# Sorting earlier and pacing attention from unit 5's first product in a one-core graph attention kernel

## The chip, the cores and the metric

The kernel runs on one NeuronCore of a Trainium2 chip. The metric is the device time of one execution in microseconds (us). Engines are called as the profile calls them: PE (TensorE, the matmul engine), DVE (VectorE), ACT (ScalarE), POOL (GpSimd) and SP (SyncE, which here only issues transfers). ACT, SP and POOL each have a DMA queue.

## What is computed

`x` has 2708 rows (nodes) of 1024 features, `adj` is a 2708 × 2708 matrix of zeros and ones, with an edge probability of 0.0014771, so that a row has about four edges.

```
h = max(layernorm(x), 0)
q = h @ W_q.T + b_q;  k = h @ W_k.T + b_k;  v = h @ W_v.T + b_v
z = (q @ k.T) / sqrt(1024) * adj
z = where(z == 0, -10000, z)
out = x + relu(softmax(z, axis=1) @ v)
```

Everything is float32.

## The kernel before

**Algebra.** `q @ k.T` is `(h @ M) @ h.T` with `M = W_q.T @ W_k / sqrt(1024)` and a bias row. So the kernel forms M, then rows `q' = h @ M + b`, and a row's scores are dot products of its q' with those few rows of h that are its neighbours. The weighted sum u of these rows of h is multiplied by `W_v.T` last, so that there are two dense stages of 2708 × 1024 × 1024 and no dense attention.

**The search.** DVE finds the columns of the ones of each row tile of `adj` (128 rows) by a search over four quarters (`found`), and `listed` turns the finds of a batch of up to four tiles into up to 16 keys per row. `counts` counts the keys, `sort` works out with two small matmuls at which position a row comes in an order by falling degree, and `put` scatters the rows' tables to that place; `reload` brings the sorted table back. Rows 0 to 1023 (tiles 0 to 7, searched last, in two batches of four) are one part, and the others, searched first, another. After the sort, tile t needs only K[t] gathered neighbours: 8 (and one row of sums kept elsewhere), 7, 5, 5, 4, 3, 3, 2 for tiles 0 to 7. Tile 21 stands for the neighbours of tiles 0 and 8 beyond the eighth, and has 7.

**Units.** The dense work is done in 20 units of two row tiles (256 rows) and one single tile. Units 0 to 9 ("q") form q' of tiles 0 to 19, units 10 to 19 ("o") form the output of the tiles in the order of attention. A unit does seven block products of the Strassen-Winograd scheme in place of eight, written by `multiply(n, results, after)` in this order (`multiply` calls `after(i)` between them, i being the step; the work of the other engines is written there):

- after steps 0 and 1: `s2` by T1 (bank Y); step 2; `a12` (bank X), then `c11`; step 3; `s4` (bank Z), then `c12`; step 4; `s3` (bank Y), then `c22`; step 5; then for the next unit `a11` and `s1` (`between` and `opened`); then `a22` (bank Y), then `c21`; step 6.

The result `c22` reads bank Y, which the `a22` product writes next. In q units of tiles 8 to 11 and in all o units but the last, ACT first copies the bank (`copied`); in the other q units DVE reads the bank itself (L1091). The operands `s1` to `s4` of unit n + 1 are sums on DVE (`blocks`: `upper` transposes the first tile, `lower` the second and does the sums, L722), written in steps 0 and 2 of unit n, and for unit 4 in steps 4 and 5 of unit 3. PE transposes the tiles, except o tiles that were stored in a turned order (`faced_tiles`), which DVE transposes (L705). A q unit's rows are gathered by POOL two units ahead (`load_rows`), and q' of tiles 8 to 19 is stored to `q_late` (L1084). Unit FIRST = 4 is the first whose rows come sorted; `last_q` is 9.

**Attention.** `attention(order)` is a generator that runs beside units 5 to 18. The order of the tiles is 6, 5, 4, 3, 2, 21, 0, 20, 7, 17, 13, 18, 12 and so on. For each tile `fetch` loads its rows of q' on POOL (L833 for tiles from 8 on, which waits for their store), `fill` gathers neighbours into the 11 buffers that are free (L610), `scores` does K[t] dot products on DVE (L863), `weights` the softmax, `sums` adds the weighted rows on DVE (L923). Scores of the next tile stand before the sums of this one where both fit into the buffers. Tile 17 has 3 neighbours, tile 20 has 1.

**Pacing.** The generator yields an estimate after each operation: 1.3 for a score or a sum, 0.6 for a tile's weights. `advance(share)` writes out operations until their estimates use up what was granted. Each step grants `share`, 20.9 / 7 in units up to 14, less 2.3 / 7 for each tile of a following o unit that DVE transposes. Before unit n + 2's rows are loaded, `advance(1.0)` goes on until its tiles are done. From unit 4 on the order of DVE alone is the written one; the order of the other engines is the scheduler's. POOL's queue is in the scheduler's order too: an instruction that can go is put ahead of one that has to wait.

**Where the change touches.** `steps_at` and `steps_ahead` say which steps of search and sort are written in which (unit, step): "j21" is `listed(21)`, the keys of the last batch, "c0" its `counts`, "o0" its `sort`, "g0" to "g4" are sums of squares on ACT, "w0-7" the scatters, "b0" the reload. `steps_ahead` are followed at the start of a step, `steps_at` near its end.

Of the kernel before, what the change touches and what calls it, by code (L numbers as in the profile page):

```python
# [65 lines left out]
def tile_preln_masked_attention(  # L66
# [147 lines left out]
    def stats(group):  # L214

        G = len(group)
        mv = stat.tile([P, 4, 2], FT, tag="mv", name="mv")
        if tiles[group[-1]][1] < P:
            nc.vector.memset(mv, 1.0)
        xs = []  # L220
        for i, t in enumerate(group):
            t0, n = tiles[t]
            if 15 <= t < 18:
                xt = work.tile([P, D], FT, tag="q", name=f"x_{t}", bufs=4)
            elif t >= FULL - 1:
                xt = work.tile([P, D], FT, tag="hT", name=f"x_{t}", bufs=2)
            else:
                xt = row_tile(f"x_{t}")
            if t < EARLY:
                kept[t] = xt  # L230
            nc.sync.dma_start(xt[:n], x[t0:t0 + n, :])
            xs.append(xt)
            if t in MOMENTS:
                continue
            st = stat.tile([P, NH, 6], FT, tag="st", name="st")
            for s in range(NH):
                nc.vector.bn_stats(st[:n, s, :], xt[:n, s * NB:(s + 1) * NB])
            nc.vector.bn_aggr(mv[:n, i, :], st[:n].rearrange("p s k -> p (s k)"))
        normed[group[0]] = group, xs, mv

    def moments(t):

        group, xs, mv = next(g for g in normed.values() if t in g[0])
        i = t - group[0]
        junk = work.tile([P, D], mybir.dt.uint8, tag="junk", name="junk_x", bufs=1)
        nc.scalar.activation(junk, xs[i], AF.Copy, scale=-1.0 / (ROOT * D), accum_out=mv[:, i, 0:1])
        nc.scalar.activation(junk, xs[i], AF.Square, scale=1.0 / ROOT, bias=mv[:, i, 0:1], accum_out=mv[:, i, 1:2])
# [3 lines left out]
    def root(first):  # L251

        group, xs, mv = normed.pop(first)
        G = len(group)
        r = stat.tile([P, 5, 4], FT, tag="r", name="r")
        mean, var = mv[:, :G, 0], mv[:, :G, 1]
        down = float(ROOT) if first in MOMENTS else -1.0
        eng = nc.gpsimd
        eng.tensor_scalar(r[:, 0, :G], var, EPS, None, op0=ALU.add)
        eng.tensor_tensor(r[:, 1, :G], r[:, 0, :G], minus[:, :G], op=ALU.pow)  # L260
        eng.tensor_tensor(r[:, 2, :G], r[:, 0, :G], r[:, 1, :G], op=ALU.mult)
        eng.tensor_tensor(r[:, 2, :G], r[:, 2, :G], r[:, 1, :G], op=ALU.mult)
        eng.tensor_scalar(r[:, 2, :G], r[:, 2, :G], -0.5, 1.5, op0=ALU.mult, op1=ALU.add)
        eng.tensor_tensor(r[:, 3, :G], r[:, 2, :G], r[:, 1, :G], op=ALU.mult)
        eng.tensor_scalar(r[:, 2, :G], mean, down, None, op0=ALU.mult)
        rooted.append(eng.tensor_tensor(r[:, 4, :G], r[:, 2, :G], r[:, 3, :G], op=ALU.mult))  # L266
        eng.tensor_scalar(msq[:, 9 + group[0]:9 + group[0] + G], r[:, 3, :G], MLIMIT / THIN, None, op0=ALU.mult)
        normed[first] = group, xs, r
# [40 lines left out]
    def follow(steps):  # L309

        for step in steps.split():
            first, *only = step[1:].split(".")
            first, *last = first.split("-")
            first = int(first or 0)
            if step[0] == "s":
                stats(range(first, int(last[0] if last else first) + 1))
            elif step[0] == "m":
                moments(first)
            elif step[0] == "r":
                root(first)  # L320
            elif step[0] == "a":
                apply(first, *[range(int(o[0]), int(o[-1]) + 1) for o in only])
            elif step[0] in "hk":
                keep(first, step[0] == "h")
            elif step[0] == "+":
                owe(first)
            elif step[0] == "p":
                counted(first)
            elif step[0] == "c":
                counts(*halves[first])  # L330
            elif step[0] == "o":
                sorted_at.append(sort(*halves[first]))
            elif step[0] == "w":
                pooled.close()
                with tc.issue_after((behind if first < EARLY else products)[-1].ins):
                    entered.append(put(first, int(last[0]) + 1))
            elif step == "z":
                pooled.enter_context(tc.manual_schedule(engines={mybir.EngineType.Pool}))
                with tc.issue_after(entered[-1].ins):
                    reload(EARLY, NT)  # L340
            elif step[0] == "b":
                reload(*halves[first])
            elif step[0] == "g":
                squared(first)
            else:
                if step[0] == "e":
                    counted(first)
                if step[0] != "j":
                    found(first, *[range(int(o[0]), int(o[-1]) + 1) for o in only])
                if step[0] != "i":  # L350
                    listed(first)
# [262 lines left out]
    rows_of = {}  # L614
    FIRST = EARLY // 2
# [147 lines left out]
    def natural_rows(n):  # L763
# [23 lines left out]
    steps_ahead = {(1, 5): "o1", (3, 6): "o0"}  # L787

    slots, free = [], []

# [217 lines left out]
    def add_block(bank, a, b, last=True):  # L1008
        for c in range(4):
            mm = nc.tensor.matmul(bank, a[:, c, :], b[:, c, :], start=False, stop=(c == 3), skip_group_check=True)  # L1010
        return mm
# [3 lines left out]
    def opened(n):  # L1015

        if n not in banks_of:
            return
        X, Z = banks_of[n]
        ops = ops_of[n][0]  # L1020
        add_block(X, ops["a11"], M[:, 0, 0])
        Y = psum.tile([P, NB], FT, tag="acc", name="psy")
        nc.scalar.copy(Y, X)
        products.append(add_block(Z, ops["s1"], T[:, 0] if units[n][0] == "q" else M[:, 0, 1]))
        p5 = small("p5")
        nc.scalar.copy(p5, Z)
        opened_of[n] = Y, p5
# [168 lines left out]
    units = [("q",) + p for p in q_pairs] + [("o",) + p for p in o_pairs]  # L1196
# [20 lines left out]
    last_q = len(q_pairs) - 1  # L1217
# [13 lines left out]
    for n, unit in enumerate(units):  # L1231
# [5 lines left out]
            nc.sync.dma_start(bp_dram, bp_sb[0:1, :])  # L1237
        turn = n in (0, FIRST - 1)
        share = (20.9 if n < len(units) - 5 else 21.5) / 7
        nxt = units[n + 1] if n + 1 < len(units) else None  # L1240
        if nxt is not None and nxt[0] == "o":
            share -= 2.3 / 7 * len(set(nxt[1:]) & faced_tiles)
# [2 lines left out]
        def after(i):  # L1245
# [4 lines left out]
            if (n, i) == (2, 5):  # L1250
# [5 lines left out]
                owe(7)  # L1256
                rows_of[FIRST + 1] = load_rows(units[FIRST + 1])
                pooled.close()
            if n == FIRST and i in (1, 4, 5):
                for g in slots[:4] if i == 1 else slots[4:6] if i == 4 else slots[6:8]:  # L1260
                    with tc.issue_after(sorted_at[-1].ins):
                        nc.vector.memset(g, 0.0)
            b11, t1, b21, b22 = M[:, 0, 0], M[:, 0, 1], M[:, 1, 0], M[:, 1, 1]
# [24 lines left out]
                marked(EARLY, NT)  # L1288
            if (n, i) == (FIRST + 2, 4):
                nc.vector.tensor_scalar(msq, msq, MLIMIT, None, op0=ALU.is_gt)  # L1290
            if n > FIRST + 1 or n == FIRST + 1 and i > 1:
                advance(share)
            if nxt is not None:

                if i == (3 if n == 0 else 4 if turn else 0):
                    ops_of[n + 1] = blocks(*rows_of[n + 1], nc.gpsimd if n + 1 < FIRST - 1 else None)
                    with tc.issue_after(products[-1].ins) if n + 1 == FIRST else nullcontext():
                        ops_of[n + 1][1]()
                if i == (4 if n == 0 else 5 if turn else 2):
                    ops_of[n + 1][2]()  # L1300
                    rows_of.pop(n + 1)
                    if n == last_q - 1:
                        all_rows()
                if i == 3:
                    banks_of[n + 1] = banks_for(bp_sb)
                if i == 6 and n + 2 < FIRST:
                    natural_rows(n + 2)
                if i == (2 if n == FIRST else 3 if n == last_q else 4) and n + 2 > FIRST and n + 2 < len(units) and n + 2 not in rows_of:
                    while units[n + 2][0] == "o" and not done.issuperset(units[n + 2][1:]):
                        advance(1.0)  # L1310
                    rows_of[n + 2] = load_rows(units[n + 2])
# [259 lines left out]
```

## Time and profile before

| | |
|---|---|
| median of 3 runs | 635.72 us |
| runs | 635.58 to 637.35 us |
| the profiled execution | 631.83 us |
| its span in the trace | 630.1 us |
| granted TensorE clock, mean | 0.999 |
| busy: PE, DVE, ACT, POOL | 619.6, 523.3, 288.4, 363.1 us |
| transfers | 182.19 MB, mean 289 GB/s |

The times of the parts below are those of the profiled execution, from the start of its span. PE is busy almost throughout: the q units take 25.8 us each with their transposes, the o units 24.0 us. Unit 3's first own product begins at 190.4 us, unit 5's at 242.9, unit 9's at 346.9 and unit 10's at 371.0. A product is eight records of matmuls (four float32 matmuls of two passes) and takes 3.43 us.

A row of the timeline gives start, duration, engine, line, operation, output and inputs with their shapes, how many, and in brackets how long the engine sat idle before it and what ended that. A row of the chain of waits gives start, duration and what it was. A row of the transfers gives what was moved, the queue, how many, the size and the time from issue to landing. `psy` is bank Y, `ps` the banks X and Z, `wlow` holds T, `pq` is a tile's q' and `g` a gathered neighbour.

### The profile page before, as it was taken

The numbers are of one execution on the slowest core, as the hardware profiler recorded it, in microseconds if no ns is written. First come the engines' busy times: TensorE is split into PE (matmuls) and PEld (weight loads), VectorE is DVE, ScalarE is ACT, GpSimd is POOL, SyncE is SP. The second block draws the span as 40 slices with busy tenths as digits, with TensorE's granted clock in tenths as the row PEclk, the third lists the DMA queues.
The fourth block names the chain that finished last, engine by engine and source line by source line (L and its number), as shares of the span: only waits on it lengthen the run. The fifth ranks groups of instructions, "written<-read, shape, count | busy, mean of one in ns | idle before, by whom it ended". The sixth has DMA issues, their size and how long they took to land.

```text
span 630.1 us, 6067 instructions
## 1 busy us (share of the span) xinstructions
PE 619.6 (98%) x1579; PEld 310.3 (49%) x1579; DVE 523.3 (83%) x1022; ACT 288.4 (46%) x421; POOL 363.1 (58%) x394
## 2 busy tenths in 40 slices
PE   8999999999999999999999998999999999999996
PEld 5777766444444444454454443444444444444442
DVE  5999879997996664887988969999997999988741
ACT  3538985749677563343341333434342323343300
POOL 2649860885778177754561632757667477852241
PEclk9999999999999999999999999999999999999999
DMA  8999997688796439997489998899999999997481
GB/s 330 407 371 326 343 354 294 209 288 326 255 387 241 166 113 319 350 379 236 154 306 325 332 359 265 235 333 346 347 318 324 344 278 305 349 284 194 103 296 71
DMA packets 65088, 182.19 MB, mean 289 GB/s; under 512 B 9959, under 2 KB 20023, under 8 KB 64408
## 3 DMA queue, kind: packets, MB, share of 16 engines
q0 software_dynamic: 26656, 86.02, 43.4%
q1 hardware_dynamic: 31594, 71.53, 32.8%
q10 hardware_dynamic: 6798, 24.20, 9.8%
q8 instruction: 14, 0.23, 0.2%
q14 instruction: 26, 0.21, 0.1%
HBM read 146.70 MB, written 43.36 MB: 302 GB/s over the span
## 4 chain that ended last, share of the span: by engine, by line
PE 56%; DMA 17%; DVE 11%; issue 9%; POOL 4%; ACT 1%; SPq 1%; POOLq 0%; DVEq 0%; ACTq 0%
PE ps L1010 22%; PE psy L1010 15%; PE ps_y L476 7%; DMA out_dram<-y,tab 5%; PE ps_x L476 4%; DMA or<-u_dram 4%; PE ps_z L476 4%; DVE junk L863 4%; PE pt L415 3%; DMA pq<-q_late 2%; DVE u L923 2%; DMA q_late<-q 2%; DMA g<-h_dram,tab 2%; DMA u_dram<-v 1%; DVE a L705 1%
## 5 line engine op out<-in xcount | busy, mean ns | idle before, releaser
L1010 PE MATMUL psy<-wlow,s 128*128 128x512 f32 x320 | 144.0, 592 | 0.0
L1010 PE MATMUL ps<-M,a 128*128 128x512 f32 x320 | 144.0, 593 | 0.0
L610 POOL DMA_INDIRECT g<-h_dram,tab x91 | 110.3, 1212 | 55.8 <-ACT u L912 19.8
L863 DVE SCALAR_TENSOR_TENSOR junk<-g,pq 128x1024 uint8<-128x1024 f32 x90 | 110.0, 1223 | 16.8 <-DMA g<-h_dram,tab 10.2
L1010 PE MATMUL ps<-M,s 128*128 128x512 f32 x240 | 108.0, 592 | 2.2 <-DVE s L722 2.2
L1010 PEld LDWEIGHTS psy<-wlow,s 128*128 128x128 f32 x320 | 59.9, 190 | 72.4 <-issue 70.2
L1010 PEld LDWEIGHTS ps<-M,a 128*128 128x128 f32 x320 | 59.9, 190 | 71.8 <-issue 71.3
L923 DVE SCALAR_TENSOR_TENSOR u<-g,coef,u 128x1024 f32<-128x1024 f32 x66 | 84.6, 1282 | 4.9 <-ACT u L912 3.5
L1010 PEld LDWEIGHTS ps<-M,s 128*128 128x128 f32 x240 | 45.4, 190 | 59.7 <-issue 58.3
L389 DVE FIND_INDEX8 at<-ones,adj 128x8 uint32<-128x685 f32 (+1 forms) x88 | 74.5, 865 | 0.0
L1010 PE MATMUL psy<-wlow,a 128*128 128x512 f32 x160 | 72.0, 593 | 0.1
L368 ACT ACTIVATE sized<-adj 128x2708 uint8<-128x2708 f32 (+1 forms) x22 | 54.3, 2466 | 7.5 <-DMA adj<-in_adj_dram 6.1
L298 POOL TENSOR_TENSOR hsum<-hsum,x 128x256 f32<-128x256 f32 (+1 forms) x56 | 38.7, 728 | 25.4 <-DVE wlow L444 22.0
L1109 POOL DMA_INDIRECT y<-in_x_dram,tab x19 | 32.2, 1696 | 31.4 <-ACT y L1126 22.4
L1010 PEld LDWEIGHTS psy<-wlow,a 128*128 128x128 f32 x160 | 30.3, 190 | 38.7 <-issue 37.3
L944 ACT COPY v<-u 128x1024 f32<-128x1024 f32 x19 | 19.9, 1045 | 48.9 <-DVE u L923 43.5
L808 POOL DMA_INDIRECT out_dram<-y,tab x21 | 27.8, 1325 | 22.0 <-issue 13.6
L1010 PE MATMUL ps<-wlow,s 128*128 128x512 f32 x80 | 36.0, 592 | 0.0
L626 POOL DMA_INDIRECT tab_dram<-tab,pos_i x22 | 21.9, 993 | 20.9 <-DVE pos_i L689 15.4
L912 ACT ACTIVATE u<-g,coef 128x1024 f32<-128x1024 f32 x18 | 20.7, 1148 | 24.2 <-DVE coef L911 24.1
L760 ACT COPY ps<-bp_sb 128x512 f32<-128x512 f32 x42 | 24.6, 595 | 11.0 <-DVE y L1144 10.3
L276 ACT ACTIVATE x<-x,r 128x1024 f32<-128x1024 f32 (+1 forms) x22 | 25.8, 1232 | 5.6 <-POOL r L266 5.6
(251 smaller groups left out, 848.5 us busy)
## 6 DMA issues: line engine op xcount, KB each, us to landing
adj<-in_adj_dram SPq DMA_DIRECT2D x21, 1354.0 KB, 11.2
x<-in_x_dram SPq DMA_DIRECT2D x21, 512.0 KB, 4.2
h_dram<-x ACTq DMA_DIRECT2D x21, 512.0 KB, 8.4
u_dram<-v ACTq DMA_DIRECT2D x19, 512.0 KB, 8.5
or<-u_dram SPq DMA_DIRECT2D x76, 128.0 KB, 9.7
q_late<-q SPq DMA_DIRECT2D x12, 512.0 KB, 9.4
pq<-q_late POOLq DMA_DIRECT2D x12, 512.0 KB, 10.5
M<-in_wv_dram SPq DMA_DIRECT2D x3, 1024.0 KB, 15.4
```

Source lines behind the costliest of these rows:

```text
L276: nc.scalar.activation(xs[i][:n], xs[i][:n], AF.Relu, bias=r[:n, 4, i:i + 1], scale=r[:n, 3, i:i + 1])
L298: small.append(nc.gpsimd.tensor_add(hsum[:n, cols], hsum[:n, cols], xt[:n, cols]))
L368: nc.scalar.activation(sized[:n], a[:n, :, :PW], AF.Abs, accum_out=total[:n, t:t + 1])
L389: nc.vector.max_index(at[:n, k - first_k, g, :], ones[:n, 0:8], a[:n, g, :])
L476: mm = nc.tensor.matmul(bank, a_tile(o + H * a[0], a[1], i), b(o), start=first and o == 0, stop=(o == H - 1), skip_group_check=True)
L610: return nc.gpsimd.indirect_dma_start(out=dst, out_offset=None, in_=src, in_offset=off, bounds_check=N - 1, oob_is_err=False)
L760: nc.scalar.copy(return_[h], row[:, h * NB:(h + 1) * NB])
L808: to = nc.gpsimd.indirect_dma_start(out=out, out_offset=bass.IndirectOffsetOnAxis(ap=ptab.bitcast(U32)[:n, t, SLOTS:SLOTS + 1], axis=0), i ...
L863: chained(lambda: nc.vector.scalar_tensor_tensor(junk, g_of[t][s], 1.0, tq[t], op0=ALU.mult, op1=ALU.mult, accum_out=zall[:, t, s:s + 1]))
L923: chained(lambda: nc.vector.scalar_tensor_tensor(u, g_of[t][s], coef[:, s:s + 1], u, op0=ALU.mult, op1=ALU.add))
L1010: mm = nc.tensor.matmul(bank, a[:, c, :], b[:, c, :], start=False, stop=(c == 3), skip_group_check=True)
L1109: return nc.gpsimd.indirect_dma_start(out=y[:n], out_offset=None, in_=x, in_offset=off, compute_op=ALU.add)
```

## The change

Six things change:

- The keys and counts of the last batch ("j21 c0") are written in step 4 of unit 3, ahead of unit 4's sums; it was step 5, behind them. The squares "g0" stay in step 5.
- The sort "o0" is written inside `opened(4)`, between unit 4's `a11` and `s1` products; it was step 6 of unit 3.
- The eight buffers cleared on DVE are all cleared in step 1 of unit 4; it was four there, two in step 4 and two in step 5.
- `advance(share)` begins with step 0 of unit 5; it was step 2.
- Unit 9 is granted 2.3 less and unit 10 4.6 less, spread over their seven steps.
- The rows of units 6 to 9 are gathered in step 2 of the unit two before; for units 7, 8 and 9 it was step 4.

```
-                (3, 1): "i21", (3, 3): "p21", (3, 5): "j21 c0 g0", (3, 6): "w0-7 g1 g2 g3 g4", (4, 4): "b0"}
-    steps_ahead = {(1, 5): "o1", (3, 6): "o0"}
+                (3, 1): "i21", (3, 3): "p21", (3, 4): "j21 c0", (3, 5): "g0", (3, 6): "w0-7 g1 g2 g3 g4", (4, 4): "b0"}
+    steps_ahead = {(1, 5): "o1"}
...
         Y = psum.tile([P, NB], FT, tag="acc", name="psy")
         nc.scalar.copy(Y, X)
+        if n == FIRST:
+            follow("o0")
         products.append(add_block(Z, ops["s1"], T[:, 0] if units[n][0] == "q" else M[:, 0, 1]))
...
         share = (20.9 if n < len(units) - 5 else 21.5) / 7
+        if n in (last_q, last_q + 1):
+            share -= 2.3 / 7 * (n - last_q + 1)
...
-            if n == FIRST and i in (1, 4, 5):
-                for g in slots[:4] if i == 1 else slots[4:6] if i == 4 else slots[6:8]:
+            if n == FIRST and i == 1:
+                for g in slots[:8]:
                     with tc.issue_after(sorted_at[-1].ins):
                         nc.vector.memset(g, 0.0)
...
-            if n > FIRST + 1 or n == FIRST + 1 and i > 1:
+            if n > FIRST:
                 advance(share)
...
-                if i == (2 if n == FIRST else 3 if n == last_q else 4) and n + 2 > FIRST and n + 2 < len(units) and n + 2 not in rows_of:
+                if i == (2 if FIRST <= n <= last_q - 2 else 3 if n == last_q else 4) and n + 2 > FIRST and n + 2 < len(units) and n + 2 not in rows_of:
```

## The prediction, made before the change was run

> **What bounds the kernel.** I read the page first, then PE's waits, PE's timeline around the one large wait, the chain that ended last before it, and VectorE (DVE), POOL and the transfers in the same stretch.
>
> ```profile
> span 630.1 us, 6067 instructions
> ...
> PE 619.6 (98%) x1579; PEld 310.3 (49%) x1579; DVE 523.3 (83%) x1022; ACT 288.4 (46%) x421; POOL 363.1 (58%) x394
> ```
>
> PE is busy for 619.6 of 630.1 us, and the change takes no product away. So it can win only what PE idles, and little of that lies in the stages that it touches:
>
> ```profile
> PE ps L1010 <- DVE s L722: 2.2, 1, 2.2
> ...
> PE ps L1010 <- DVE T_alone L705: 0.8, 1, 0.8
> ```
>
> ```profile
> 357.22 3.60 PE L1010 MATMUL psy<-wlow,s 128*128 128x512 f32 x8
> ...
> 367.52 3.60 PE L1010 MATMUL psy<-wlow,a 128*128 128x512 f32 x8
> ...
> 384.68 3.60 PE L1010 MATMUL ps<-M,a 128*128 128x512 f32 x8
> 390.44 3.67 PE L1010 MATMUL ps<-M,s 128*128 128x512 f32 x8 [2.16 <-DVE s L722]
> ```
>
> A product is eight such records, 3.43 us from one to the next. 357.22 is unit 9's `s3` product, 367.52 its `a22` product (the last of unit 9), 390.44 the `s1` product of unit 11, begun inside unit 10, which waited 2.16 us for VectorE's `s1`. That wait is all that a faster VectorE can give. Why was VectorE late? The chain says:
>
> ```profile
> 343.65 3.45 PE psy L1010 x8
> ...
> 347.73 10.06 DMA q_late<-q
> ...
> 357.83 0.47 issue
> ...
> 358.32 13.95 DMA pq<-q_late
> ...
> 372.38 0.09 DVE junk L863
> ```
>
> ```profile
> 365.73 0.68 DVE L1091 TENSOR_TENSOR q<-psy,p 128x512 f32<-128x512 f32 x1
> 366.33 1.22 DVE L863 SCALAR_TENSOR_TENSOR junk<-g,pq 128x1024 uint8<-128x1024 f32 x1
> ...
> 372.38 1.23 DVE L863 SCALAR_TENSOR_TENSOR junk<-g,pq 128x1024 uint8<-128x1024 f32 x1 [3.64 <-DMA pq<-q_late]
> ...
> 389.60 0.69 DVE L722 TENSOR_TENSOR s<-a,s 128x512 f32<-128x512 f32 x1
> ```
>
> Tile 17's q is made by unit 8's last product (ends 347.1), stored until 357.8, loaded again until 372.3. VectorE stood 3.64 us at tile 17's first score for it. So VectorE's lateness at 390 is not mere load: it is a transfer that starts at a time which PE sets, and which more VectorE time cannot hasten. Note what stands just ahead of that score: L1091 at 365.73, which reads unit 9's bank Y (`c22`), so that the `a22` product may write it at 367.52.
>
> **The change, part by part.** The search's end, the sort, the memsets:
>
> ```profile
> 200.92 0.69 DVE L1094 TENSOR_TENSOR q<-ps,u 128x512 f32<-128x512 f32 x1 [1.58 <-issue]
> ...
> 206.23 1.29 DVE L722 TENSOR_TENSOR s<-a,pt 128x512 f32<-128x512 f32 x2 [0.36 <-ACT a L718]
> ...
> 208.76 0.28 DVE L402 TENSOR_TENSOR cand<-first,at 128x128 f32<-128x128 f32 x1
> ...
> 213.27 0.22 DVE L669 TENSOR_SCALAR tab<-keys 128x128 uint32<-128x128 f32 x1
> 216.48 0.31 DVE L682 COPY sort<-ps_all 128x144 f32<-128x144 f32 x1 [2.99 <-PE ps_all L680]
> ...
> 218.79 0.17 DVE L689 CAST pos_i<-deg 128x8 uint32<-128x8 f32 x1
> 219.11 0.91 DVE L1262 MEMSET g<- 128x1024 f32 x1 [0.15 <-issue]
> ...
> 224.68 1.29 DVE L722 TENSOR_TENSOR s<-a,pt 128x512 f32<-128x512 f32 x2 [1.43 <-issue]
> ```
>
> ```profile
> 209.28 3.60 PE L1010 MATMUL ps<-wlow,s 128*128 128x512 f32 x8
> ```
>
> Keys and counts take 213.49 − 208.76 = 4.7 us. In front of unit 3's `c22` and unit 4's `s1`, they run from 201.6 to 206.3, into idle time; `c22` follows until 207.0, `s1` is done at 207.7, and PE wants it at 209.28: no cost while 1.6 us of cover last. The sort's two matmuls only change place; they read counts ready by 206.3. Should PE take them before unit 4's `a11` product, which begins 3.43 us ahead of 209.28, it could lose 206.3 − 205.85, so 0 to 0.5 us; I take 0. From the copy of the counts to the positions VectorE takes 218.96 − 216.48 = 2.5 us; begun at 209.7 it ends near 212.2 in place of 218.96, so POOL's puts, SP's reload and tile 6's gathers move up by up to 6.7 us. The eight memsets together (about 1.07 us each from start to start, from 212.3) end near 221, before the sums of 224.68: nothing. The rows of q gathered two steps sooner issue the same transfers; POOL's queue has them 2 × 1.3 us ahead of row gathers that stood before them, while
>
> ```profile
> 309.42 1.39 POOL L612 DMA_INDIRECT qr<-h_dram,tab  x1 [0.30 <-issue]
> ```
>
> ```profile
> qr<-h_dram,tab POOLq DMA_INDIRECT x1, 4.7
> ```
>
> ```profile
> 319.42 1.04 PE L415 MATMUL pt<-ident,qr 128*128 128x128 f32 x8
> ```
>
> the one issued at 309.4 landed 4.7 us later, at 314.1, for transposes at 319.4. The rows had 5 us to spare and get more: 0; 2.6 us more on POOL for a gather of the planner I price with the scores below.
>
> Attention from unit 5's first step:
>
> ```profile
> 240.75 1.23 DVE L863 SCALAR_TENSOR_TENSOR junk<-g,pq 128x1024 uint8<-128x1024 f32 x1 [5.17 <-DMA g<-h_dram,tab]
> ...
> 248.05 1.28 DVE L722 TENSOR_TENSOR s<-a,pt 128x512 f32<-128x512 f32 x2 [3.21 <-ACT a L718]
> ```
>
> ```profile
> 260.98 3.60 PE L1010 MATMUL ps<-wlow,s 128*128 128x512 f32 x8
> ```
>
> Scores begin between 234 (all 6.7 us gained) and 240.75 (none gained). By the planner's arithmetic below, seven scores and sums and one tile's weights then stand before the sums of 248.05, where three scores did: even from 240.75 and with 2.6 us of POOL's queue in between, those sums begin by 240.75 + 2.6 + 7 × 1.3 + 0.6 = 253.1; PE wants the first at 260.98. Cost 0, and VectorE goes into units 6 to 9 up to 6 us ahead.
>
> Now the shares. What attention does at which step follows from the planner: a score or a sum counts 1.3, a tile's weights 0.6, and an operation is written out at the first step where the granted sum exceeds what stands before it. Before tile 17's first score stand 37 scores, 30 sums and 8 weights: 67 × 1.3 + 8 × 0.6 = 91.9. Before the change, units 5 to 8 grant 26 steps of 20.9 / 7 = 2.986, unit 9 steps of 16.3 / 7 = 2.329: 91.6 after step 5, 93.9 after step 6. So the score comes in step 6, behind `c22` (written between steps 4 and 5), as the trace shows. With the change, units 5 to 8 grant 28 steps = 83.6, and unit 9 steps of (16.3 − 2.3) / 7 = 2.0: 91.6 after step 3, 93.6 after step 4. The first two scores of tile 17 (the second needs 93.2) come in **step 4, ahead of `c22`**. VectorE keeps the written order; c22 of this unit reads the bank itself (the copy by ScalarE is for tiles 8 to 11), and PE's `a22` product waits behind it.
>
> So at unit 9: with tile 17's q landed at time T, two scores (2 × 1.23) and L1091 (0.68) with gaps end at T + 3.2, and `a22` starts then if that is after 367.52. The stall is T − 364.3. What is T? The store still starts at 347.7: PE sets it.
>
> ```profile
> 346.92:370.95 24.03, 24.03 (x57) 10.64 (x56) 20.92 (x32) 9.62 (x14) 13.69 (x13) 1.00 1.03 332
> ```
>
> ```profile
> 346.53 1.00 POOL L610 DMA_INDIRECT g<-h_dram,tab  x1 [0.30 <-issue]
> ...
> 352.88 1.49 POOL L610 DMA_INDIRECT g<-h_dram,tab  x1 [0.30 <-issue]
> 358.32 0.57 POOL L833 DMA_DIRECT2D pq<-q_late  x1 [3.95 <-DMA q_late<-q]
> ...
> 398.54 0.59 POOL L833 DMA_DIRECT2D pq<-q_late  x1
> ```
>
> ```profile
> g<-h_dram,tab POOLq DMA_INDIRECT x1, 11.1
> ```
>
> ```profile
> g<-h_dram,tab POOLq DMA_INDIRECT x1, 16.8
> ```
>
> ```profile
> pq<-q_late POOLq DMA_DIRECT2D x1, 512.0 KB, 6.5
> ```
>
> The first row's last three columns are PE's clock, the DMA share and GB/s: the DMA engines are full in unit 9 (1.03). The gather issued at 346.5 took 11.1 us, that of 352.9 took 16.8 and landed at 369.7, the load of 358.3 at 372.3: POOL's transfers land in the order of issue, and the load stood behind two gathers of tile 13 that had been put ahead of it. A like load of 398.5, with little before it, took 6.5 us. Lower end: 358.3 + 6.5 = 364.8. Upper end: the change frees tile 0's buffers some 6 us sooner, so that up to three more gathers of tile 13 are free to go ahead of the load while POOL waits for the store; at (369.7 − 357.6) / 4 = 3.0 us each less the 6 us head start, 372.3 + 3 = 375. I take 372.3, the row itself: more ahead of it, but sooner.
>
> The Trainium skill (DMA: Bandwidth & Descriptors, Queues, rings and completion order) says that an engine starts a queue's descriptors in ring order and takes turns between queues. By it gathers moved up go ahead of the load and T stays late (372.3: a stall of 8.0 us); were a load free to overtake, T would be 364.8 and the stall 0.5. The landings above agree with the order.
>
> Does the old wait go? From T to the end of unit 11's `s1` VectorE took 390.3 − 372.3 = 18.0 us; now L1091 (0.7), tile 17's weights (0.5) and one more score (1.2) are in it: T + 20.4. PE wants it after six products from T + 3.2: T + 23.8. So it goes.
>
> **Sum**, against the profiled execution (631.83 us, span 630.1): + 8.0 at unit 9's `a22`, − 2.2 at unit 11's `s1`, 0 elsewhere: + 5.8. The profiled execution lies 3.9 us under the median of 635.72, whose runs go from 635.58 to 637.35; I add the difference to the median: 641.5 us.
>
> **Rivals.** *The load comes early.* If tile 13's gathers stay behind the load and the gathers before it have landed, T is at most 364.3: `a22` never waits, the 2.2 us are won, 633.5. For it: the head start of 6 us, and the share taken from units 9 and 10. Against: the store's end at 357.8 leaves 6.5 us, the shortest load that I saw. It decides at T = 364.3; chance 0.12. *The load lands in between*, T from 364.6 to 368.4: stall 0.3 to 4.1, net − 1.9 to + 1.9, 633.8 to 637.6. For it: fewer gathers go ahead than I think. Chance 0.18. *The early start doesn't happen*, as the reload or the first gathers land no sooner: VectorE then enters unit 6 behind by up to 6 us. The order written out is the same, so the stall at `a22` is as in the forecast, 641.5; this is inside its chance, as is T of 375 (a stall of 10.7, 644.2).
>
> **How the numbers follow.** About 0.3% (1.9 us) is what a measurement of this kernel can tell from no change. Forecast with its late end 0.70, in between 0.18, early 0.12. The range goes from 634.0 (nearly all of the middle case) to 645.5 (T at 376, one gather's share later than the bound); what it leaves out is mainly the early case. The forecast's own range is 637.6 to 645.5.
>
> **What would show it.** In the changed profile: the scores of tile 17 stand before unit 9's L1091; one of them waits some 10 us for pq from q_late; PE's `psy<-wlow,a` after 364 waits for L1091 for about 8 us; the wait on L722 is gone; positions near 212, first score between 234 and 241. I am wrong if the load of tile 17 lands before 364.6, if PE has no wait there, or if another wait on PE is over 2 us.

## The result and the profile after

| | before | after |
|---|---|---|
| median | 636.2 us (20 runs) | 634.35 us (20 runs) |
| lowest and highest | 633.38, 639.99 | 632.27, 636.52 |
| the profiled execution, its span | 631.83, 630.1 | 635.63, 633.9 |
| granted clock in it | 0.999 | 0.994 |

The ratio is 0.997, with a 95% interval of 0.9956 to 0.9985: the change wins some 1.9 us (0.3%), where the prediction had a loss of 5.8. Disturbed runs are left out of all ratios here. A ratio is an estimate from the single runs, with its interval, and not the quotient of the two medians; below the two differ by up to 0.0021.

The head of the page of the kernel after:

```profile
span 633.9 us, 6066 instructions
...
PE 623.0 (98%) x1579; PEld 312.0 (49%) x1579; DVE 525.2 (83%) x1022; ACT 291.6 (46%) x421; POOL 370.7 (58%) x394
```

PE does the same 1579 records and is busy for 3.4 us more (619.6 before); that is taken up under what was not expected. PE's waits after, in us, times, longest:

```profile
PE pt L415 <- DMA qr<-h_dram,tab: 2.1, 1, 2.1
PE ps L1010 <- DMA M<-in_wv_dram: 2.0, 1, 2.0
PE ps_y L511 <- POOL hsum L121: 1.2, 1, 1.2
```

Both waits that the prediction listed are gone: unit 11's `s1` (2.2) and the single tile's transposes (0.8). Two others are there. The second is at unit 10's `a11` product, which waits for a block of W_v. PE, SP and DVE of the kernel after around it:

```profile
361.30 3.60 PE L1010 MATMUL psy<-wlow,s 128*128 128x512 f32 x8
...
366.93 5.37 PE L1010 MATMUL ps<-M,a 128*128 128x512 f32 x8 [2.03 <-DMA M<-in_wv_dram]
...
375.57 3.60 PE L1010 MATMUL psy<-wlow,a 128*128 128x512 f32 x8
```

```profile
351.81 0.34 SPq L1086 DMA_DIRECT2D q_late<-q  x1
352.25 0.38 SPq L1271 DMA_DIRECT2D wlow<-in_wv_dram  x1
352.95 5.44 SPq L1271 DMA_DIRECT2D M<-in_wv_dram  x2
```

```profile
371.21 1.23 DVE L863 SCALAR_TENSOR_TENSOR junk<-g,pq 128x1024 uint8<-128x1024 f32 x1 [2.95 <-DMA pq<-q_late]
372.48 1.22 DVE L863 SCALAR_TENSOR_TENSOR junk<-g,pq 128x1024 uint8<-128x1024 f32 x1
373.63 0.69 DVE L1093 TENSOR_TENSOR q<-psy,p 128x512 f32<-128x512 f32 x1
```

Three things are to be seen. The planner's sum was right: two scores of tile 17 stand ahead of L1093 (L1091 before), as worked out. The product that must wait for it, `a22` at 375.57, shows no wait: the wait for the weights, two products earlier, and the 5.37 us of the product behind that wait had already pushed it behind 373.63 + 0.69 = 374.3. And SP's queue is in another order. Of the same transfers SP before showed:

```profile
340.25 0.33 SPq L1267 DMA_DIRECT2D M<-in_wv_dram  x1
...
343.68 0.33 SPq L1267 DMA_DIRECT2D wlow<-in_wv_dram  x1
347.73 0.32 SPq L1084 DMA_DIRECT2D q_late<-q  x1
```

Before, both W_v blocks were asked for ahead of tile 17's store; after, behind it, and so 12.7 and 8.6 us later, of which 4.1 are this execution's own shift (the store itself is 4.1 later).

### The profile page after: what moved, and what is told of

Same layout as the page of the kernel before. It is cut to its first block, busy times and chain, and to the rows that moved or that the text cites. A ratio compares the mean times of both kernels' runs of the same rounds, so it can differ in the third digit from the quotient of the medians.

```text
span 633.9 us, 6066 instructions
## 1 busy us (share of the span) xinstructions
PE 623.0 (98%) x1579; PEld 312.0 (49%) x1579; DVE 525.2 (83%) x1022; ACT 291.6 (46%) x421; POOL 370.7 (58%) x394
## 4 chain that ended last, share of the span: by engine, by line
PE 96%; DMA 3%; issue 0%; POOL 0%; SPq 0%; DVE 0%; ACT 0%; POOLq 0%
PE ps L1010 44%; PE psy L1010 32%; PE ps_y L476 6%; PE ps_x L476 4%; PE ps_z L476 4%; PE pt L415 3%; DMA M<-in_wv_dram 2%; DMA qr<-h_dram,tab 1%; PE ps_y L511 1%; PE ps_h L1226 0%; PE ps_v L594 0%; DVE y_alone L1391 0%; POOL out_dram L1375 0%; ACT q L1101 0%; POOLq L1397 0%
## 5 line engine op out<-in xcount | busy, mean ns | idle before, releaser
L610 POOL DMA_INDIRECT g<-h_dram,tab x93 | 120.5, 1296 | 62.7 <-ACT u L912 21.7
L1010 PE MATMUL ps<-M,a 128*128 128x512 f32 x320 | 145.8, 599 | 2.0 <-DMA M<-in_wv_dram 2.0
L863 DVE SCALAR_TENSOR_TENSOR junk<-g,pq 128x1024 uint8<-128x1024 f32 x92 | 112.4, 1221 | 11.8 <-issue 4.9
L923 DVE SCALAR_TENSOR_TENSOR u<-g,coef,u 128x1024 f32<-128x1024 f32 x70 | 89.7, 1281 | 5.5 <-ACT u L912 4.0
L1111 POOL DMA_INDIRECT y<-in_x_dram,tab x19 | 34.6, 1821 | 35.6 <-ACT y L1128 24.2
L626 POOL DMA_INDIRECT tab_dram<-tab,pos_i x22 | 21.7, 985 | 11.2 <-DVE pos_i L689 5.7
L912 ACT ACTIVATE u<-g,coef 128x1024 f32<-128x1024 f32 x16 | 18.4, 1149 | 21.3 <-DVE coef L911 13.2
```

The source lines that it names most:

```text
L610: return nc.gpsimd.indirect_dma_start(out=dst, out_offset=None, in_=src, in_offset=off, bounds_check=N - 1, oob_is_err=False)
L863: chained(lambda: nc.vector.scalar_tensor_tensor(junk, g_of[t][s], 1.0, tq[t], op0=ALU.mult, op1=ALU.mult, accum_out=zall[:, t, s:s + 1]))
L923: chained(lambda: nc.vector.scalar_tensor_tensor(u, g_of[t][s], coef[:, s:s + 1], u, op0=ALU.mult, op1=ALU.add))
L1111: return nc.gpsimd.indirect_dma_start(out=y[:n], out_offset=None, in_=x, in_offset=off, compute_op=ALU.add)
```

## The experiments

After the result there were two theories. **The swap:** the change removes the waits for `s1` and for the single tile, and pays for it with the late weights; the stall at `a22` is real, but hidden behind the weights' wait. **The rival:** the stall isn't there, and the gain comes from sorting and attention that run earlier, with the weights' wait an accident beside it. Each of the three groups below ran on one chip, beside the kernel before (medians 632.66, 635.9 and 633.54 us); ratios are to it.

| kernel | median, us | ratio | 95% interval |
|---|---|---|---|
| before, again | 633.22 | 1.0006 | 0.9991 to 1.0022 |
| after, again | 631.37 | 0.9979 | 0.9963 to 0.9994 |
| after, grants as before | 635.39 | 1.0044 | 1.003 to 1.0058 |
| before, lower grants alone | 629.74 | 0.9947 | 0.9926 to 0.9968 |
| after, weights first | 636.77 | 1.0002 | 0.9982 to 1.0021 |
| after, weights first and copy | 633.53 | 0.9967 | 0.9944 to 0.999 |
| after, copy alone | 633.39 | 0.996 | 0.9939 to 0.9981 |
| before, sort sooner alone | 635.53 | 0.9975 | 0.9953 to 0.9996 |
| before, lower grants alone, again | 630.12 | 0.9953 | 0.9934 to 0.9972 |
| after, weights first and copy, again | 629.39 | 0.9955 | 0.9933 to 0.9977 |
| after, weights first, gathers behind | 628.0 | 0.9924 | 0.9898 to 0.995 |
| after, weights first, grants 4.8 and 2.1 | 631.4 | 0.9974 | 0.9956 to 0.9993 |

### Both kernels again on one chip

Unchanged kernels, for two traces side by side.

> The kernel before, unchanged, for a second trace. Theory A (waits that differ from execution to execution hide the order of VectorE): the second trace shows a wait on PE that the first did not have, as for unit 4's gathered rows (2 to 4 us with the slow matmuls behind it), and a time near 636. Theory B (the order of VectorE alone decides): the waits are those of the first trace, 2.2 us for unit 11's first sum, and nothing else over 1 us. Ratio to the kernel before 1.000 in both.

> The changed kernel, unchanged, for a second trace. Theory A: PE waits for rows or weights at other places or for other times than in the first trace; where unit 4's rows are in time, PE reaches unit 9's last product earlier and waits there 1 to 5 us for the result of bank Y that stands behind tile 17's scores. Theory B: the same two waits of 2 us each as in the first trace and none for bank Y. Ratio to the kernel before 0.997 in both.

PE's waits of the kernel before, and of the kernel after:

```profile
PE ps L1010 <- DVE s L722: 2.6, 1, 2.6
...
PE ps L1010 <- DVE T_alone L705: 0.9, 1, 0.9
PE psy L1010 <- DVE q L1091: 0.3, 1, 0.3
```

```profile
PE ps L1010 <- DMA M<-in_wv_dram: 2.2, 1, 2.2
PE ps_y L511 <- POOL hsum L121: 1.2, 1, 1.2
```

The start's 1.2 us stand in both. The rest falls from 2.6 + 0.9 + 0.3 = 3.8 to 2.2, by 1.6; the spans fall from 631.4 to 629.7, by 1.7; the medians by 1.85. So on one chip the waits account for the gain. For before, theory B holds. For after neither holds whole: unit 4's rows are in time, as A allows, but the wait for bank Y that A expects is hardly there. PE and DVE of this second trace of after:

```profile
363.65 3.67 PE L1010 MATMUL ps<-M,a 128*128 128x512 f32 x8 [2.22 <-DMA M<-in_wv_dram]
...
370.88 3.70 PE L1010 MATMUL psy<-wlow,a 128*128 128x512 f32 x8
```

```profile
367.72 1.23 DVE L863 SCALAR_TENSOR_TENSOR junk<-g,pq 128x1024 uint8<-128x1024 f32 x1 [2.74 <-DMA pq<-q_late]
...
370.14 0.69 DVE L1093 TENSOR_TENSOR q<-psy,p 128x512 f32<-128x512 f32 x1
```

With the weights in time, `a22` would be due at 363.65 − 2.22 + 2 × 3.43 = 368.3; L1093 lets it go at 370.8. The order's stall is there, 2.5 us, but the weights' 2.2 lie over all but 0.3 of it. It is 2.5 and not 8.0 because tile 17's q came at 367.7, and not at 372.3. POOL of this trace and the row of tile 17's load show what stood ahead of it:

```profile
345.03 1.02 POOL L610 DMA_INDIRECT g<-h_dram,tab  x1 [0.30 <-issue]
...
350.52 1.73 POOL L610 DMA_INDIRECT g<-h_dram,tab  x1 [0.53 <-DVE u L929]
356.41 1.15 POOL L833 DMA_DIRECT2D pq<-q_late  x2 [4.16 <-DMA q_late<-q]
```

```profile
pq<-q_late POOLq DMA_DIRECT2D x1, 512.0 KB, 11.3
```

From 345.03 to 350.52 five gathers are issued, tile 13's; the kernel that holds tile 13's gathers back, further down, issues none between 343.8 and its load.

### The grants alone, and everything but the grants

```
+        if n in (last_q, last_q + 1):
+            share -= 2.3 / 7 * (n - last_q + 1)
```

One kernel is the kernel after without these two lines, the other the kernel before with them.

> The changed kernel without the lower grants of units 9 and 10. By the planner's sums tile 17's first score then stands in step 3 of unit 9, ahead of the results of banks Z and Y. Theory A (the order of VectorE at unit 9 costs what tile 17's q is late): PE waits for bank Y at unit 9's last product by 3 us or more, VectorE is late in unit 10 again, and the kernel is 3 to 8 us slower than the changed one. Theory B (the lower grants matter only through VectorE's load in units 9 and 10): 2 to 3 us slower than the changed one, with PE's wait at a first sum of unit 11, not at bank Y.

> The kernel before with the lower grants of units 9 and 10 alone. Tile 17's first score then stands in step 0 of unit 10, behind both results of unit 9. Theory A: no wait at unit 9 and none at unit 11's first sum, 2 us faster than before, unless the work put off (6.9 us of VectorE) comes back as a wait near units 16 and 17, where the planner is made to go on by 7 steps. Theory B (the gain of the change needs the earlier start): no faster than before, as the work put off costs PE 2 us or more at unit 16 or 17.

Everything but the grants is slower than before, 1.0044: in its trace the W_v loads stand behind tile 17's store again, and PE waits 1.9 for the weights (and the next product takes 5.37 us), 1.0 for L1093 at `a22` (theory A: 3 or more), and 1.7 for ScalarE at 522 us, which itself stood for an output transfer. The grants alone are the best of the four: 0.9947. Its waits on PE, all of them:

```profile
PE ps_y L511 <- POOL hsum L121: 1.2, 1, 1.2
PE ps L1010 <- DVE T_alone L705: 0.9, 1, 0.9
```

and DVE in units 9 and 10:

```profile
364.33 0.68 DVE L1091 TENSOR_TENSOR q<-psy,p 128x512 f32<-128x512 f32 x1
...
373.08 1.23 DVE L863 SCALAR_TENSOR_TENSOR junk<-g,pq 128x1024 uint8<-128x1024 f32 x1 [1.65 <-DMA pq<-q_late]
...
384.45 0.69 DVE L722 TENSOR_TENSOR s<-a,s 128x512 f32<-128x512 f32 x1
```

Tile 17's q lands no sooner than before (373.1), but its score is written in unit 10, behind L1091, and fewer scores stand ahead of unit 11's sums: they begin at 384.45, and `s1` no longer waits. This speaks against the rival: attention that runs earlier isn't needed for the gain, and by itself it costs.

### The weights first, and the copy of bank Y

The loads of the two W_v blocks are issued inside `opened(9)`, each behind the product that frees its place, and tile 17's store behind both. The two loads that the kernel issued for these blocks go (lines left out are marked `...`):

```
         add_block(X, ops["a11"], M[:, 0, 0])
+        if n == last_q:
+            weights_in.append(nc.sync.dma_start(M[:, 0, 0], of_wv(0, 0)))
...
+        if n == last_q:
+            weights_in.append(nc.sync.dma_start(T[:, 0], of_wv(1, 1)))
...
-            (nc.scalar if t < 4 else nc.sync).dma_start(dst, q)
+            with tc.issue_after(weights_in[-1].ins) if t == BARE - 3 else nullcontext():
+                (nc.scalar if t < 4 else nc.sync).dma_start(dst, q)
...
-            for at, place, src in (((-2, 0), t1, of_wv(0, 0)), ((0, 0), T[:, 0], of_wv(1, 1)), ((0, 0), b11, of_wv(0, 0)),
-                                   ((0, 3), b21, of_wv(1, 0))):
+            for at, place, src in (((-2, 0), t1, of_wv(0, 0)), ((0, 3), b21, of_wv(1, 0))):
```

The copy lets ScalarE take bank Y over in unit 9, so that `a22` needn't wait for DVE:

```
-            behind.append(nc.vector.tensor_add(qb[:, hi], copied(Y) if EARLY <= ta < EARLY + 4 else Y, p5))
+            behind.append(nc.vector.tensor_add(qb[:, hi], copied(Y) if EARLY <= ta < EARLY + 4 or ta == BARE - 2 else Y, p5))
```

> The changed kernel, with the two loads of W_v's blocks for unit 10 put back ahead of tile 17's store in SP's queue (issued near 340 and 344 us, as in the kernel before). Theory A (SP's new order causes PE's wait of 2 us for the weights, and that wait hides VectorE's order): the wait for the weights is gone, tile 17's store lands some 10 us after its issue in place of 7.5, its load some 5 us later, and PE waits 3 to 8 us for bank Y at unit 9's last product; 1 to 6 us slower than the changed kernel. Theory B (the weights are late by the crowd of gathers, whatever SP's order): the wait for the weights stays at 1 to 2 us, time as the changed kernel.

> The same, and in unit 9 ScalarE copies bank Y before VectorE reads it, so that PE need not wait for VectorE there. Theory A: no wait over 1 us on PE between 100 us and 600 us; span near 628, 2 us faster than the changed kernel and 3 to 4 us faster than the kernel before. Theory B: the wait for the weights stays, time as the changed kernel within 1 us. A third possibility: VectorE, held by tile 17's scores, is late for unit 11's sums, 2 us or more.

> The changed kernel with the copy of bank Y in unit 9 alone. Theory A: the wait for the weights (2.0 to 2.2 us) stays, and the copy changes nothing, since the result of bank Y is done when PE comes: the changed kernel's time within 0.7 us. Theory B (bank Y decides): 2 us or more faster than the changed kernel.

With the weights first alone the gain is gone, 1.0002. Its trace has SP's old order, no wait for the weights, and a wait at `a22`. SP and PE:

```profile
342.58 0.35 SPq L1023 DMA_DIRECT2D M<-in_wv_dram  x1
346.01 0.35 SPq L1030 DMA_DIRECT2D wlow<-in_wv_dram  x1
350.06 0.33 SPq L1091 DMA_DIRECT2D q_late<-q  x1
```

```profile
373.11 3.70 PE L1010 MATMUL psy<-wlow,a 128*128 128x512 f32 x8 [3.09 <-DVE q L1098]
```

The chain of waits of this kernel, and then DVE, name why (L1098 is L1093 of the kernel after):

```profile
350.06 8.16 DMA q_late<-q
...
358.75 11.18 DMA pq<-q_late
```

```profile
369.95 1.22 DVE L863 SCALAR_TENSOR_TENSOR junk<-g,pq 128x1024 uint8<-128x1024 f32 x1 [5.23 <-DMA pq<-q_late]
...
372.36 0.69 DVE L1098 TENSOR_TENSOR q<-psy,p 128x512 f32<-128x512 f32 x1
```

This is the prediction's mechanism laid bare: store, load, two scores, L1098, `a22`, with a wait of 3.1 us where it had 8.0. With the copy as well both waits are away, and the time is 0.9967 and, in the last group, 0.9955. The first trace with both still has three other waits of 1.3 us (unit 4's rows, ScalarE at 257 us, the single tile), against theory A; the one of the last group has none of them. The copy alone leaves the weights' wait (2.1 in its trace) and measures 0.996, which its interval doesn't separate from the one with both. The kernel after as it is was not run in this group.

### The sort sooner, alone

The kernel before with only the edits of keys, sort and memsets.

> The kernel before with keys, counts and sort sooner and the buffers cleared together, pacing, grants and row gathers as before. Theory A: positions near 212 us and tile 6's first score up to 6 us sooner in VectorE's timeline, and PE's wait for unit 11's first sum (2.2 to 2.6 us) as before, since it hangs on tile 17's load: ratio to the kernel before 0.999 to 1.001. Theory B (an earlier sort puts VectorE ahead by itself): the wait goes, 2 us faster.

0.9975, with an interval that just leaves out 1, while the medians differ by 0.06% only: at most a small gain. Its trace keeps SP's old order and the wait at unit 11's `s1`:

```profile
395.37 5.14 PE L1010 MATMUL ps<-M,s 128*128 128x512 f32 x8 [2.52 <-DVE s L722]
```

So the sort edits alone don't turn SP's order. Neither do the grants alone, whose traces have the old one, and the kernel after without the grants has the new one. What is left is the pacing from unit 5's step 0 or the row gathers, alone or together with the sort; they weren't run apart.

### The grants again, beside the repaired kernels

> The kernel before with the lower grants of units 9 and 10 alone, a second time and beside the three below on one chip. Theory G (the gain of the change is the removed wait for unit 11's s1, 2.2 to 2.6 us, and the single tile's transposes, 0.9; its price is the weights' loads that come later, about 2): the lower grants move tile 17's first score into unit 10 and leave the order of SP's transfers as it was, so both PE waits of the change are absent and the 2.2 to 2.6 us are won: 0.994 to 0.997, and PE has no wait over 1.5 us in units 9 and 10. Rival R (the first measurement, 0.9947 from six runs, was chance, and the gain needs the earlier attention): 0.998 to 1.001, with a wait for the s1 of unit 11 or 12 of 1 us or more.

> The kernel after with the two W_v loads issued ahead of tile 17's store and bank Y copied by ScalarE in unit 9, a second time. Theory G: neither of the change's two new waits is left, so this version should equal the lower grants alone within 0.002, that is 0.994 to 0.997, and no PE wait over 1.5 us between 340 and 400 us. Rival R (the earlier attention has a price of its own outside units 9 to 11): it is slower than the lower grants alone by 0.002 or more, at or above 0.998.

0.9953 and 0.9955, both as the swap expects. In the repaired kernel's trace no wait on PE is over 1.2 us; in that of the grants alone:

```profile
PE ps_y L511 <- POOL hsum L121: 1.2, 1, 1.2
PE ps L1010 <- DVE T_alone L705: 0.8, 1, 0.8
```

Six edits with two repairs reach what two lines of the change reach alone.

### The gathers of tile 13 behind tile 17's load

The weights first, without the copy, and

```
-                with tc.issue_after(first_q[0].ins) if first_q else nullcontext():
+                late = held_q if t == 13 else first_q
+                with tc.issue_after(late[0].ins) if late else nullcontext():
```

where `held_q` holds tile 17's load.

> The kernel after with the W_v loads first (without the copy of bank Y), and the gathers of tile 13 issued only behind tile 17's load of q. Theory A (the load stands in POOL's queue behind the gathers of tile 13 that go ahead of it): the load takes 6.5 to 8 us from issue to landing in place of 11.2, tile 17's first score starts 3 us sooner, near 366.5, and PE's wait of 3.1 us at unit 9's a22 product falls to 0 to 0.5; time 2 to 3 us under the variant with the weights first alone. Theory B (the transfers only share the bandwidth, and the order of issue doesn't matter): the load still takes 10 to 11 us, the wait at a22 stays near 3, and the time is that of the weights first alone, about 1.000.

The best of all, 0.9924: 627.32 to 628.53 us in 5 runs, where the grants alone gave 629.41 to 631.75 in 11 on the same chip. PE's only wait in it is the 1.2 at the start. POOL, the load's row among the transfers (KB, us to landing), and DVE:

```profile
343.77 1.02 POOL L610 DMA_INDIRECT g<-h_dram,tab  x1 [0.30 <-issue]
355.32 1.15 POOL L833 DMA_DIRECT2D pq<-q_late  x2 [10.54 <-DMA q_late<-q]
```

```profile
pq<-q_late POOLq DMA_DIRECT2D x1, 512.0 KB, 8.8
```

```profile
364.27 1.22 DVE L866 SCALAR_TENSOR_TENSOR junk<-g,pq 128x1024 uint8<-128x1024 f32 x1 [1.27 <-DMA pq<-q_late]
```

No gather is issued between 343.8 and 355.3. The load takes 8.8 us in place of 11.2 (expected by theory A: 6.5 to 8, by B: 10 to 11), and the score starts at 364.27 (in the variant without this, 369.95). It isn't the order in POOL's queue alone: the store, which goes through SP's queue, was also sooner done, 355.32 − 348.39 = 6.9 us from its issue to the load's, against 358.75 − 350.06 = 8.7. Some 2.4 us come from the load, 1.8 from the store. The ratio lies 0.0078 under that of the weights first alone, some 5 us and more than theory A's 2 to 3; the two ratios are of two chips, and what makes up the rest isn't shown. The Trainium skill (DMA: Bandwidth & Descriptors, Queues, rings and completion order) has an engine start a ring's descriptors in order and take turns between rings. That fits both parts, but no run here separates them further.

### Less in unit 9, more in unit 10

The weights first, and the same 6.9 us taken as 4.8 and 2.1, so that tile 17's score falls behind L1098:

```
-            share -= 2.3 / 7 * (n - last_q + 1)
+            share -= (4.8 if n == last_q else 2.1) / 7
```

> The kernel after with the W_v loads first, and with the 6.9 us that are taken from units 9 and 10 divided 4.8 and 2.1 in place of 2.3 and 4.6. Planner's sum: 83.6 granted through unit 8, then 1.64 a step: 91.8 after step 4, 93.5 after step 5, so tile 17's first score is written in step 5 of unit 9, behind the line that reads bank Y. Theory C (the stall at a22 is only a matter of that order): no wait of a22 for VectorE, no wait for the weights, no copy on ScalarE needed; time 0.995 to 0.997, as with the copy. Rival D (VectorE comes late elsewhere, since the grants of unit 10 are higher by 2.5): the wait for the s1 sums of unit 11 returns with 1 to 2.5 us; time 0.998 to 1.001.

Theory C holds in unit 9: no wait for the weights, none at `a22`, though tile 17's q came at 369.9. The time, 0.9974, is rival D's, but not its mechanism: `s1` doesn't wait. PE waits late in the kernel instead, and ScalarE, named by the first of these waits, had itself stood for an output transfer:

```profile
493.65 3.70 PE L1010 MATMUL psy<-wlow,s 128*128 128x512 f32 x8 [1.47 <-ACT psy L1025]
607.20 3.70 PE L1010 MATMUL ps<-M,T_alone 128*128 128x512 f32 x8 [1.67 <-DVE T_alone L705]
```

```profile
492.48 0.63 ACT L1129 ACTIVATE y<-p 128x512 f32<-128x512 f32 x1 [8.31 <-DMA out_dram<-y,tab]
```

Whether the moved grants cause these, over 100 us later, stays open.

## Why the prediction was wrong, step by step

- **What the kernel wins: right, a little small.** The 2.2 us at `s1` were won (2.6 in the second trace of before), and 0.8 to 0.9 at the single tile beside them, which the sum had as 0 under "0 elsewhere". That wait comes and goes among the variants, without a cause found here.
- **The written order at `a22`: right.** Two scores of tile 17 stand ahead of L1093 in both traces of after. Where nothing else held PE, `a22` waited for L1093 3.1 us.
- **The time T of tile 17's q: the step that failed, and with it the one big term of the sum.** The prediction took "372.3, the row itself", of a transfer "which more VectorE time cannot hasten". Measured: 367.7 in the second trace of after, where the store took 7.5 us (348.34 to 355.9) for the row's 10.06, and the load came 11.3 us after its issue at 356.41 for 13.95. Five gathers of tile 13 did go ahead of the load, as feared; but they were issued from 345.0 to 350.5, and the first four took 6.6, 7.2, 9.8 and 13.0 us, where the two rows quoted in the prediction took 11.1 and 16.8. The mistake was to keep a row's landing time when the change moved the transfers ahead of it. From the issue of the store to tile 17's first score it is 24.7 to 26.1 us in the five traces without the new pacing and row gathers (before twice, the grants alone twice, the sort alone), and 19.1 to 21.3 in eight with them, whether SP has the weights ahead of the store or behind it. So earlier work on VectorE did hasten the transfer, unless it was the earlier row gathers. The stall was 2.5 to 3.1 us and not 8.0. With 2.5 in its place, and the 3.8 won in place of 2.2, the sum is −1.3, near the −1.7 of the spans.
- **The rival "in between": its range (T from 364.6 to 368.4) holds what happened, its reason doesn't.** Not fewer gathers went ahead of the load, but as many as the forecast had, and sooner. By its own sum T = 367.7 gives 3.4 − 2.2 = + 1.2; the measured −1.9 is lower mainly through the larger wins and an `a22` that was due 0.8 us later (368.3 for 367.52).
- **"0 elsewhere": a second step that failed.** "The store still starts at 347.7: PE sets it" is right of the store. It was not asked what else in SP's queue would change its place. The change turned the scheduler's order, the W_v loads went behind the store, and PE waited 2.0 to 2.2 us for them. This new wait is what hid the stall, so that no wait shows at `a22` in the first trace. It hardly moved the time, since of two costs that overlap only the longer is paid. With the weights first the stall stands alone and nothing of the gain is left: 1.0002 (that trace also has 1.7 us of wait for unit 4's rows).
- **Sort, memsets, row gathers, early start: 0 where the prediction looked, right.** The positions came at 213.0 in the second trace of after (forecast: near 212), the first score at 238.95 in the first (forecast: 234 to 241). In the second trace the sort's matmul (L680) stands at 209.91, between `a11` and `s1`, and PE doesn't wait there. But the turned order of SP comes from the pacing or the row gathers.
- **The base.** The sum was a difference added to a median, and that held: spans differ by 1.7 and medians by 1.85 on one chip. The single profiles don't: 631.83 before and 635.63 after would say the opposite. The upper end of the range doesn't follow from its reason: T at 376 gives 645.2, and one gather's share (3.0) past 375 would be 378.

## What to carry to other kernels

When a change moves work between steps, list every queue whose order the scheduler may turn by it, and for each transfer that gets behind another one, who waits for it; a queue of loads without computation, like SP's here, is the one that is easily left out. Two new waits at neighbouring products can cost the larger one and not the sum, as 2.2 and 2.5 us did here, so that removing one of them shows the other (1.0002 with the weights first) and not a gain. A transfer's landing time, read from a trace, holds only as long as the change leaves the transfers ahead of it where they were. And before a bundle of edits is kept, run the cheapest of them alone: two lines of the six edits gave 0.995, and the full set only 0.997 to 0.998.

## What was not expected of the hardware

**A wait on PE can cost twice.** In the trace of after the product behind the wait for the weights took 5.37 us and not 3.60, and the granted clock (third from the right) in that stretch was 0.68; in unit 3, behind the wait for the gathered rows, it was 0.72:

```profile
203.00:209.00 6.00, 6.00 (x16) 3.23 (x17) 5.49 (x25) 1.17 (x2) 5.84 (x9) 0.72 0.27 107
366.90:372.30 5.40, 5.37 (x9) 2.38 (x10) 2.45 (x3) 0.00 (x0) 3.37 (x3) 0.68 1.02 347
```

PE of that stretch of unit 3:

```profile
202.98 1.54 PE L415 MATMUL pt<-ident,qr 128*128 128x128 f32 x8 [2.08 <-DMA qr<-h_dram,tab]
204.32 4.85 PE L1010 MATMUL psy<-wlow,s 128*128 128x512 f32 x8
```

Against 1.04 and 3.60 elsewhere these are 0.50 + 1.25 + 1.77 = 3.5 us: the 3.4 that PE is busier than before. It isn't so each time. In the second trace of after the same wait (2.22) is followed by 3.67 us, and in the one with the weights first a wait of 3.09 by 3.70. In all 14 traces PE has ten waits of 1.9 to 3.1 us; slow products follow five of them. The Trainium skill (TensorE: Matmul & The Clock Gate, What's actually happening) says that the clock is halved after an idle window of about 3.4 us, and that the windows run freely. Here a wait of 2.0 us was enough at times, and one of 3.1 not always; that the window's position decides is not shown by any run here.

**The runs' spread goes with it in part.** Of the kernel with the weights first, two runs with a mean clock of 1.0 took 633.36 (the one traced) and 634.38 us, and nine with 0.989 to 0.997 took 635.33 to 638.18. All 11 runs of the grants alone in the last group have a clock of 0.998 or more and lie within 2.3 us. But of the 29 runs of the kernel before beside them, which spread over 7.6 us, the 10 with such a clock still go from 628.87 to 635.94: the clock isn't all of it. So what a wait costs on average is read from many runs and not from one trace.

**The rows of unit 4** (L415, 2.1 us in the trace of after) come late in some executions: that wait, of 1.3 to 2.2 us, is in the first trace of after and in all four traces of the second group, but in none of the eight traces of the other two groups. The two traces of after are of one and the same kernel, and POOL issues the first of these gathers at 197.56 in one and at 192.68 in the other. All five traces with the wait have the earlier sort, and none of the four without the earlier sort has it; the second group has no trace without it. So whether the sort takes part is open.
